# The last five spans of each layer of a two-layer GNN: edge rows added from SBUF pair by pair, one node stage between pairs, slot sums in one portion

## The chip, the cores and the metric

The kernel runs on one core of one Trainium2 chip. The metric is the device time of one execution in microseconds, taken as the median of several executions. The core has a matrix engine (TensorE, shown as PE, its weight loads as PEld), a vector engine (VectorE, DVE), an activation engine (ScalarE, ACT), GpSimd (POOL), which issues the indirect DMAs here, and SyncE (SP), which issues the other DMAs. Each engine works through its own queue in program order and waits on semaphores for the others. Tiles live in SBUF (128 partitions) or in PSUM, the banks that PE accumulates into.

## The reference

The graph has 6250 nodes and 106250 directed edges (50000 drawn, their reverses, and one loop per node), sorted by destination. A row has 256 float32.

```python
# layer 0
msg = relu(x[src] + edge_attr)
agg = segment_sum(msg, dst)
h = x + (x + agg)
f = gelu(bn1(h) @ W1.T + b1) @ W2.T + b2
x = layernorm(x + bn2(h + f))
# layer 1
h = gelu((x[src] + edge_attr) @ W1m + b1m)
agg = segment_sum(h @ W2m + b2m, dst) / max(deg, 1)
u = gelu(agg @ W1u + b1u) @ W2u + b2u
x = layernorm(x + layernorm_gamma_beta(x + u))
```

## The kernel before

**Tiles, spans, blocks.** The edges make 831 tiles of 128. Eight tiles are a span; there are V = 104 spans, 0 to 103, of which the last has seven tiles, the last of them with 10 rows. A span is two groups `g` of four tiles, a group two pairs `q`; so a span has four pairs, each a 128x512 operand. The 6250 nodes make 26 blocks of mostly 256 nodes. The last two, 24 and 25, have 128 and 96. A block is full when the last span with one of its edges has been summed: blocks 20 to 25 are full with spans 88, 92, 96, 100, 102 and 103.

**What is done to a span.** `gather` (L829) issues eight indirect DMAs from POOL, one a tile, which bring the row of each edge's source into `rings[v % 5]`, one of five ring buffers. The edge rows `ea` come by plain DMAs on SP's queue, three spans ahead (AHEAD). In layer 0 these are the raw edge features and the gathered rows those of x. In layer 1 the gathered rows are `proj` = (layer 0's result) @ W1m + b1m, and the edge rows needed are edge_attr @ W1m. The product is taken for the first group of every span during layer 0 and kept in DRAM (`zst`), and for the second group in layer 1 itself (`turned` L843/L848, `product` L856). The spans that are treated outside the steps, and the first three, have both groups' products ready in DRAM (`products_ahead`, `zst1`), and their edge rows can be added as they are. `one_hots` (L907, DVE, eight instructions) marks for each edge which of 32 slots its node has; `add_to_gathered` (L884, DVE) adds edge rows to gathered rows; `activated` or `activated_pair` (L892, L898, ACT) applies relu or gelu; `into_slots` (L927, PE) multiplies by the one-hots and so sums edges into slots; `kept_slots` (L946, ACT) copies the sums to SBUF; `slot_nodes` (L916, DVE) and `into_blocks` (L966, L974, PE) spread the slots over the nodes of the blocks, in `acc`.

**What is done to a full block.** A generator runs the node work in stages, and the list `running` holds those that are not finished. `nodes_0` is begun with two copies of `acc` (L1018 ACT, L1023 DVE) and the DMA of the degrees; its stages are: 1, W1 and gelu (L1029, L1034); 2, W2, residuals and statistics (L1042, L1047, L1052, L1054); 3, layernorm and the DMA of x1 (L1002, L1003, L1007); 4, the transpose (L1066, L1069); 5, the product with W1m, the add of b1m to `y` (L1075, L1079) and the DMA to `proj` (L1084, and L1086 for the last two blocks). `nodes_1` is begun with the division by the degree (L1347); its stages are A and B (L1357, L1362, L1367), the residuals (L1331, L1335), C (L1378, L1382 and statistics), D (L1388, L1392 and statistics), and E (the last scaling and the DMA to `out`, L1400).

**Order.** The order is written out by hand and kept. Spans 0 to 100 are gathered in steps (`step_0`, `step_1`): a step gathers span v, adds and activates span v-1, sums the second group of v-2, spreads v-3 and advances the running blocks. In the steps ACT lifts the edge rows into PSUM (`lifted`, L867) and DVE adds from there. Behind the steps come `end_0` and `end_1`. For spans 100 to 102, `late_step` calls `summed`: all one-hots, then four pairs raised into PSUM by PE against an identity (`raised`, L875, 16 matmuls of 256 columns), four adds, four activations, then the slot sums pair by pair with `further()`, which advances every running block by a stage, ahead of pairs 1 and 3. Then comes another `further()` and the spreading of the span (`full`).

**Between the layers.** Layer 1's gathers need `proj`. The gathers of its spans 0 to 2 read only `proj[:near+1]`, the rows of blocks 0 to 23, so they wait for the y of block 23. The rows of blocks 24 and 25 are added afterwards: `where(i)` loads the source numbers of one group into `tiles` or `off` and DVE builds a one-hot `z` from it (L1250), and `completed` multiplies that with y of blocks 24 and 25 and adds. The gathers from span 3 on read all of `proj` and wait for the y of block 25. Behind `full_0(103)`, `end_0` issues `where(0)`, `where(1)`, the stages of blocks 24 (`other`) and 25 (`last`) in turn, and in between `added(0)`, the lift and add of layer 1's span 0.

**Ring.** A gather into a ring buffer waits for the slot sums of the span five before.

Of the kernel before, what the change touches and what calls it, by code (L numbers as in the profile page):

```python
# [15 lines left out]
D = 256  # L16
# [11 lines left out]
RING = 5  # L28
ROW = 260
AHEAD = 3  # L30
LATE = 3
FIRST = 64


# [471 lines left out]
def kernel(  # L506
# [141 lines left out]
    with (  # L648
# [17 lines left out]
        def work():  # L666
            return psw.tile([P, 2, D], F32, name="workP")
# [199 lines left out]
                nc.scalar.copy(ps[:n, j:k, :], of[:n, q + j : q + k, :])  # L867
            return ps

        def raised(v, g, q, of):  # L870

            pair = tiles_of(v, g)[q : q + 2]
            ps = work()
            for j, n in enumerate(pair):
                nc.tensor.matmul(  # L875
                    ps[:n, j, :], lhsT=ident[:n, :n], rhs=of[:n, q + j, :], start=True, stop=True
                )
            return ps

        def add_to_gathered(v, g, q, ps):  # L880
            at = g * G + q
            r = rings[v % RING]
# [50 lines left out]
        def slot_bank():  # L933
            return pss.tile([P, 2 * D], F32, name="slotP")
# [222 lines left out]
                nc.sync.dma_start(out=zst[v], in_=zs.pop(v).rearrange("p j d -> p (j d)"))  # L1157
            advance(late)

        QUADS = [(g, q) for g in range(GROUPS) for q in range(0, G, 2)]  # L1160

        def summed(v, width, func, between=lambda i: None):

            one_hots(v)
            slot_nodes(v)
            its = [i for i in QUADS if tiles_of(v, i[0])[i[1] :]]
            rows = [raised(v, g, q, eas[v, g]) for g, q in its]
            for (g, q), ps in zip(its, rows):
                add_to_gathered(v, g, q, ps)
                activated_pair(v, g, q, func)  # L1170
            ps = slot_bank()
            for i, (g, q) in enumerate(its):
                between(i)
                at = g * G + q
                slots_of(v, width, ps, range(at, at + len(tiles_of(v, g)[q : q + 2])))
            kept_slots(v, ps, width)

        def further():
            advance(list(running))

        def late_step(v, full, func, width):

            u = v - 1
            if v == V - LATE:
                full(u - 2)
                activated(u - 1, 1, func)
                slot_nodes(u - 1)
                kept_slots(u - 1, into_slots(u - 1, width), width)
                further()
                full(u - 1)  # L1190
            summed(u, width, func, lambda i: further() if i % 2 else None)
            further()
            full(u)

        def kept_of(v):

# [33 lines left out]

        wheres = []

        def added(v):
            for g, q in QUADS:
                add_to_gathered(v, g, q, lifted(v, g, q, eas[v, g]))

        def where(i):

            to = check.tile([P, T], F32, name=("tiles", "off")[i % 2])[:, : G * P]
            nc.sync.dma_start(
                out=to,
                in_=src_rows[i * G : (i + 1) * G, :].rearrange("t e -> (t e)")[None, :]
                .to_broadcast([P, G * P]),
            )
            hot = ep.tile([P, G, D], F32, name="z", bufs=2).rearrange("p g d -> p (g d)")
            hot = hot.rearrange("p (b e) -> p b e", e=G * P)
            for b in range(len(LAST)):
                nc.vector.tensor_scalar(  # L1250
                    hot[:, b, :], to, -float(near + sum(LAST[:b])), place,
                    op0=ALU.add, op1=ALU.is_equal,
                )
            wheres.append(hot)
# [13 lines left out]
        def end_0():  # L1268

            d = V - 1  # L1270
            for v in range(V - LATE, V):
                gather(v, x, src_sb)
                late_step(v, full_0, AF.Relu, D + 1)
            other = list(running)[-1]
            assert len(running) == 1 and len(farther) == 0
            for v in range(AHEAD):
                gather(v, proj[: near + 1, :], src_near)
                load_1(v)
            summed(d, D + 1, AF.Relu, lambda i: further() if i % 2 == 0 else None)
            full_0(d, acc_work)  # L1280
            last = list(running)[-1]
            assert len(running) == 2
            advance([last])
            for i in (0, 1):
                where(i)
            for _ in range(3):
                advance([other])
                advance([last])
            added(0)
            further()  # L1290
            further()
            assert not running and len(farther) == len(LAST)
            added(1)


# [153 lines left out]
            prepared[b] = nodes_1(b, *its, bank, True)  # L1449
            next(prepared[b])  # L1450

        def full_1(v, bank=node_work, last=False):
            for b in into_blocks(v, acc_1, opened_1):
                if last:
                    gen = prepared.pop(b)
                else:
                    gen = nodes_1(b, acc_1[b], x1s.pop(b), degs_1.pop(b), invs.pop(b), bank, last)
                del acc_1[b]
                begun(b, gen)
            invert()  # L1460

        def step_1(v):
            u, w, full = v - 1, v - 2, v - 3
            if v + AHEAD < V:
                load_1(v + AHEAD)
            if AHEAD <= v:
                gather(v, proj, src_1)
            some, early_edges = AHEAD <= u, 0 <= u < AHEAD
            if early_edges:
# [12 lines left out]
            if some:  # L1482
                add_to_gathered(u, 0, 0, lifted(u, 0, 0, eas[u, 0]))
                add_to_gathered(u, 0, 2, lifted(u, 0, 2, eas[u, 0]))
            if early_edges:
                completed(u, 0)
                if u + 1 < AHEAD:
                    where(2 * u + 2)
            advance(early)
            if some:  # L1490
                add_to_gathered(u, 1, 0, product(*first))
            if early_edges:
                completed(u, 1)
                if u + 1 < AHEAD:
                    where(2 * u + 3)
            if 0 <= u:
                activated(u, 0, AF.Gelu)
            if 0 <= w < V:
                slot_nodes(w)
                kept_slots(w, into_slots(w, D), D)  # L1500
            if some:
                add_to_gathered(u, 1, 2, product(*second))
            advance(late)

        def end_1():

            d = V - 1
            for v in range(V - LATE, V):
                gather(v, proj, src_1)
                if v == V - 1:  # L1510
                    for b, bank in zip(sorted(acc_1), (node_work, acc_work)):
                        prepare(b, bank)
                late_step(v, lambda u: full_1(u, last=u == d - 1), AF.Gelu, D)
            assert len(running) == 1
            other = running[0]
            summed(d, D, AF.Gelu, lambda i: further() if i < 3 else None)
            full_1(d, last=True)
            last = running[-1]
            advance([last])
            advance([last])  # L1520
            while running:
                advance(list(running))

        begin()
        for v in range(AHEAD):
# [5 lines left out]
        for v in range(V - LATE):  # L1531
            step_0(v)
            beside.get(v, lambda: None)()
            if v > 8 and v % 2:
                next(ahead_0, None)
        assert next(ahead_0, "none") == "none"
        end_0()
        for v in range(V - LATE):
            step_1(v)
# [64 lines left out]
```

## Time and profile before

| What | Value |
|---|---|
| median of 3 runs | 2167.87 us (2167.82 to 2168.67) |
| profiled execution | 2165.82 us |
| its span in the trace | 2163.9 us |
| mean granted TensorE clock | 0.968 |
| PE busy | 1903.9 us (88%) |
| DVE busy | 1451.8 us (67%) |
| ACT busy | 1341.3 us (62%) |
| POOL busy | 1583.8 us (73%) |

The profile is one execution; it is 1.9 us longer than its span, as time lies around the first and last recorded instruction. Its page lists the busy time of each engine, the span in 40 slices, the chain of waits that ended last and the costliest groups of instructions. In a group's line `out<-in` names the tiles, `x` the count, and the figures behind the bar are busy time, mean ns of one, and idle time ahead of them with what ended most of it.

The last sums of a span into slots leave for SBUF in `kept_slots` (L946). In the trace this copy ends, for spans 98 to 103, at 1010.7, 1016.8, 1031.4, 1047.75, 1059.5 and 1071.4 us in layer 0, and at 2076.5, 2082.5, 2098.7, 2117.2, 2132.3 and 2146.9 us in layer 1. The last DVE instruction ends at 2158.6 us, the span 5.3 us after that.

### The profile page before, as it was taken

The numbers are of one execution on the slowest core, as the hardware profiler recorded it, in microseconds if no ns is written. First come the engines' busy times: TensorE is split into PE (matmuls) and PEld (weight loads), VectorE is DVE, ScalarE is ACT, GpSimd is POOL, SyncE is SP. The second block draws the span as 40 slices with busy tenths as digits, with TensorE's granted clock in tenths as the row PEclk, the third lists the DMA queues.
The fourth block names the chain that finished last, engine by engine and source line by source line (L and its number), as shares of the span: only waits on it lengthen the run. The fifth ranks groups of instructions, "written<-read, shape, count | busy, mean of one in ns | idle before, by whom it ended". The sixth has DMA issues, their size and how long they took to land.

```text
span 2163.9 us, 38059 instructions
## 1 busy us (share of the span) xinstructions
PE 1903.9 (88%) x12071; PEld 1472.0 (68%) x12071; DVE 1451.8 (67%) x4205; ACT 1341.3 (62%) x2153; POOL 1583.8 (73%) x1671
## 2 busy tenths in 40 slices
PE   5999999998998989898779998898888988888886
PEld 3777767776776777666557776677766766766654
DVE  6677766776776667666366766676676766666665
ACT  3577766676766666665336766665665666666653
POOL 7777777777777777777567777777777777777770
PEclk9999999999999999999989999999999999999998
DMA  9889888888988898887568777777777767777650
GB/s 335 263 290 323 293 294 290 292 287 286 301 289 283 287 295 281 286 288 243 174 206 267 225 244 233 221 238 243 227 227 228 242 213 235 219 233 227 212 167 26
DMA packets 318430, 541.75 MB, mean 250 GB/s; under 512 B 37260, under 2 KB 234125, under 8 KB 318093
## 3 DMA queue, kind: packets, MB, share of 16 engines
q1 hardware_dynamic: 237773, 319.65, 44.3%
q0 software_dynamic: 79744, 217.71, 32.6%
q8 instruction: 99, 1.62, 0.3%
q10 hardware_dynamic: 704, 1.87, 0.2%
q14 instruction: 110, 0.90, 0.1%
HBM read 461.90 MB, written 77.18 MB: 249 GB/s over the span
## 4 chain that ended last, share of the span: by engine, by line
PE 21%; DMA 12%; DVE 8%; issue 6%; ACT 4%; POOL 3%; DVEq 0%; ACTq 0%; POOLq 0%
DMA ring<-proj,dst_sb 11%; PE workP L856 8%; POOL ring L829 3%; PE slotP L927 3%; DVE ring L884 2%; PE nodeP L1378 2%; PE acc L966 2%; PE nodeP L1357 2%; DVE hot L907 2%; PE workP L843 1%; DVE uT L1362 1%; ACT ring L892 1%; ACT L1002 1%; PE workP L1262 1%; ACT workP L867 1%
## 5 line engine op out<-in xcount | busy, mean ns | idle before, releaser
L829 POOL DMA_INDIRECT ring<-in_x_dram,src_sb x831 | 789.0, 949 | 255.6 <-issue 137.3
L829 POOL DMA_INDIRECT ring<-proj,dst_sb x807 | 769.9, 954 | 252.8 <-issue 152.3
L856 PE MATMUL workP<-w1m_sb,eaT 128*128 128x256 f32 x3324 | 830.0, 395 | 67.8 <-DVE ring L884 45.4
L884 DVE TENSOR_TENSOR ring<-workP,ring 128x512 f32<-128x512 f32 x844 | 557.2, 684 | 426.8 <-DMA ring<-in_x_dram,src_sb 126.0
L856 PEld LDWEIGHTS workP<-w1m_sb,eaT 128*128 128x128 f32 x3324 | 621.1, 195 | 237.2 <-DVE ring L884 58.3
L892 ACT ACTIVATE ring<-ring 128x1024 f32<-128x1024 f32 x400 | 424.8, 1062 | 147.7 <-DVE ring L884 144.7
L848 ACT COPY eaT<-workP 128x512 f32<-128x512 f32 x416 | 223.8, 585 | 262.7 <-PE workP L843 261.6
L867 ACT COPY workP<-ea 128x512 f32<-128x512 f32 x606 | 334.0, 595 | 32.0 <-DVE ring L884 30.6
L966 PE MATMUL acc<-hot,sums 128*128 128x161 f32 (+22 forms) x1376 | 225.1, 296 | 91.5 <-DVE hot L960 48.9
L907 DVE TENSOR_SCALAR hot<-ramp,slot 128x32 f32<-128x32 f32 x1662 | 268.1, 259 | 0.2 <-PE slotP L927 0.2
L966 PEld LDWEIGHTS acc<-hot,sums 128*128 128x128 f32 x1376 | 187.0, 195 | 110.6 <-DVE hot L960 53.9
L927 PE MATMUL slotP<-ring,hot 128*32 128x257 f32 (+1 forms) x3324 | 248.6, 388 | 12.0 <-ACT ring L892 6.2
L843 PE MATMUL workP<-ident,ea 128*128 128x128 f32 x1584 | 212.3, 276 | 15.8 <-DMA ea<-in_edge_attr_dram 8.6
L843 PEld LDWEIGHTS workP<-ident,ea 128*128 128x128 f32 x1584 | 186.2, 142 | 41.1 <-issue 10.6
L927 PEld LDWEIGHTS slotP<-ring,hot 128*32 128x32 f32 x3324 | 97.7, 109 | 129.2 <-issue 63.3
L946 ACT COPY sums<-slotP 128x257 f32<-128x257 f32 (+1 forms) x208 | 75.4, 362 | 134.4 <-PE slotP L927 134.4
L1367 ACT ACTIVATE uT<-uT,cols_sb 128x256 f32<-128x256 f32 (+3 forms) x104 | 45.8, 487 | 132.5 <-DVE uT L1362 132.4
L1357 PE MATMUL nodeP<-fT,w 128*128 128x256 f32 (+2 forms) x400 | 101.5, 400 | 25.6 <-DVE y L1392 25.2
L1357 PEld LDWEIGHTS nodeP<-fT,w 128*128 128x128 f32 x400 | 77.9, 204 | 45.6 <-DVE y L1392 32.1
L1002 ACT ACT_TABLE_LOAD x73 | 93.7, 1283 | 1.3
L1378 PE MATMUL nodeP<-w2u_sb,uT 128*128 128x256 f32 (+1 forms) x392 | 89.3, 381 | 1.4 <-DVE y L1335 1.4
L1156 DVE COPY z<-workP 128x512 f32<-128x512 f32 x101 | 69.1, 684 | 20.7 <-PE workP L856 20.0
(154 smaller groups left out, 1582.5 us busy)
## 6 DMA issues: line engine op xcount, KB each, us to landing
ea<-in_edge_attr_dram SPq DMA_DIRECT2D x103, 1024.0 KB
ea<-zst SPq DMA_DIRECT2D x110, 512.0 KB
zst<-z SPq DMA_DIRECT2D x101, 512.0 KB
ea<-in_edge_attr_dram SPq DMA_DIRECT2D x97, 512.0 KB
ring<-in_x_dram,src_sb POOLq DMA_INDIRECT x831
ring<-proj,dst_sb POOLq DMA_INDIRECT x807
xb<-in_x_dram SPq DMA_DIRECT2D x23, 256.0 KB
x1d<-x SPq DMA_DIRECT2D x23, 256.0 KB
```

Of the source, the lines that this page charges most:

```text
L829: nc.gpsimd.indirect_dma_start(out=rings[v % RING][:n, j, :D], out_offset=None, in_=table, in_offset=bass.IndirectOffsetOnAxis(ap=rows[:n, ...
L843: nc.tensor.transpose(pe[:, j, k, :n], ea[:n, at + j, k * P : (k + 1) * P], ident[:n, :n])
L848: nc.scalar.copy(eaT[:, j:k, :, :n], pe[:, j:k, :, :n])
L856: nc.tensor.matmul(ph[:n, j, :], lhsT=eaT[:, j, k, :n], rhs=w1m_sb[:, k, :], start=(k == 0), stop=(k == KC - 1),)
L867: nc.scalar.copy(ps[:n, j:k, :], of[:n, q + j : q + k, :])
L884: nc.vector.tensor_add(r[:n, at + j : at + k, :D], ps[:n, j:k, :], r[:n, at + j : at + k, :D])
L892: nc.scalar.activation(at, at, func)
L907: nc.vector.tensor_scalar(hots[v][:n, j, :], ramp[:n, :SLOTS], slot[:n, t : t + 1], None, op0=ALU.is_equal,)
L927: nc.tensor.matmul(ps[q * SLOTS : (q + 1) * SLOTS, :width], lhsT=hot[:n, j, :], rhs=r[:n, j, :width], start=(i == 0), stop=(i == PAIR - 1 ...
L966: nc.tensor.matmul(acc[b][:, k, cols], lhsT=its[:, k * P : (k + 1) * P], rhs=at, start=(begins and k == 0), stop=(last_span[b] == v and k ...
L1357: nc.tensor.matmul(ps[:, o - i, :width], lhsT=w12[:, k, o * P : (o + 1) * P], rhs=mT[:, k, :width], start=(k == 0), stop=(k == KC - 1),)
L1378: nc.tensor.matmul(ps[:n, h, :], lhsT=uT[:, k, h * n : (h + 1) * n], rhs=w2u_sb[:, k, :], start=(k == 0), stop=(k == UC - 1),)
```

## The change

LATE goes from 3 to 4, so the steps end with span 99, and the spans 99 to 103 of each layer are treated in a new function, `late_spans`. In it

- `raised`, the PE matmuls that put edge rows into PSUM, is gone; DVE adds the edge rows from SBUF, a pair at a time, with the pair's activation behind it;
- behind each pair `between` runs one stage of the oldest running block (`stage`); behind pair 0 first `full` of the span before, behind pair 3 first the one-hots of the next span;
- the slot sums of a span come in one portion behind its four pairs (`into_slots`);
- the gather of span v+1 is issued ahead of the pairs of span v;
- in layer 0 `where` is split into its DMA (`where`) and its one-hots (`whose`); the loads 0 and 1 go out in the last step but one, and those behind them in span 100 and in layer 1's step 1;
- in layer 0 `added(0)` comes behind the last stage of blocks 24 and 25, and these two alternate by themselves;
- in layer 1 `prepare`, the residuals of blocks 24 and 25, goes behind pairs 2 and 3 of span 102, and the last stages of both blocks alternate;
- one more span per layer has its second group's product made ahead: `products_ahead` makes 14 pairs in layer 0 instead of 12 and 10 in layer 1 instead of 8, one phase of a pair in every odd step.

```diff
-LATE = 3
+LATE = 4
...
-        def raised(v, g, q, of):
...
-        def summed(v, width, func, between=lambda i: None):
-
-            one_hots(v)
-            slot_nodes(v)
-            its = [i for i in QUADS if tiles_of(v, i[0])[i[1] :]]
-            rows = [raised(v, g, q, eas[v, g]) for g, q in its]
-            for (g, q), ps in zip(its, rows):
-                add_to_gathered(v, g, q, ps)
-                activated_pair(v, g, q, func)
-            ps = slot_bank()
-            for i, (g, q) in enumerate(its):
-                between(i)
-                at = g * G + q
-                slots_of(v, width, ps, range(at, at + len(tiles_of(v, g)[q : q + 2])))
-            kept_slots(v, ps, width)
-
-        def further():
-            advance(list(running))
...
+        def stage():
+
+            if running:
+                advance(running[:1])
+
+        def late_spans(load, table, rows, full, func, width, between, behind=lambda v: None):
+
+            v = V - LATE
+            for u in range(v + AHEAD, V):
+                load(u)
+            gather(v, table, rows)
+            full(v - 3)
+            activated(v - 2, 1, func)
+            slot_nodes(v - 2)
+            kept_slots(v - 2, into_slots(v - 2, width), width)
+            one_hots(v - 1)
+            for v in range(V - LATE - 1, V):
+                if v + 1 < V:
+                    gather(v + 1, table, rows)
+                for i, (g, q) in enumerate(PAIRS):
+                    if tiles_of(v, g)[q:]:
+                        add_to_gathered(v, g, q, eas[v, g][:, q : q + 2, :])
+                        activated_pair(v, g, q, func)
+                    if i == 0:
+                        full(v - 1)
+                    if i == 3 and v + 1 < V:
+                        one_hots(v + 1)
+                    between(v, i)
+                slot_nodes(v)
+                kept_slots(v, into_slots(v, width), width)
+                behind(v)
...
+            def between(v, i):
+                if v == V - LATE and i > 1:
+                    whose()
+                    where(i)
+                if v < d or i < 2:
+                    stage()
...
+            late_spans(load_0, x, src_sb, full_0, AF.Relu, D + 1, between, behind)
+            full_0(d, work)
+            other, last = running
             advance([last])
-            for i in (0, 1):
-                where(i)
-            for _ in range(3):
+            for _ in range(2):
                 advance([other])
                 advance([last])
+            advance([other])
+            advance([last])
+            advance([last])
+            assert not running and len(farther) == len(LAST)
             added(0)
-            further()
-            further()
             added(1)
...
+            def between(v, i):
+                if v == d - 1 and i > 1:
+                    prepare(sorted(acc_1)[i - 2], work)
+                elif v < d or i < 3:
+                    stage()
+
+            late_spans(load_1, proj, src_1, lambda v: full_1(v, v >= d - 1), AF.Gelu, D, between)
+            full_1(d, True)
+            other, last = running
+            for gen in (last, last, other, last, other, last, last):
+                advance([gen])
```

More of the change, by code (lines that the diff above doesn't have):

```diff
@@ L868, in lifted @@
             return ps
-        def raised(v, g, q, of):
[L872 to L878, printed above, removed]
         def add_to_gathered(v, g, q, ps):
@@ L1158, in step_0 @@
             advance(late)
-        QUADS = [(g, q) for g in range(GROUPS) for q in range(0, G, 2)]
-        def summed(v, width, func, between=lambda i: None):
-            one_hots(v)
-            slot_nodes(v)
-            its = [i for i in QUADS if tiles_of(v, i[0])[i[1] :]]
-            rows = [raised(v, g, q, eas[v, g]) for g, q in its]
-            for (g, q), ps in zip(its, rows):
-                add_to_gathered(v, g, q, ps)
-                activated_pair(v, g, q, func)
-            ps = slot_bank()
-            for i, (g, q) in enumerate(its):
-                between(i)
-                at = g * G + q
-                slots_of(v, width, ps, range(at, at + len(tiles_of(v, g)[q : q + 2])))
-            kept_slots(v, ps, width)
@@ L1178, in further @@
-        def further():
-            advance(list(running))
[L1181 to L1188, printed above, removed]
-                further()
-                full(u - 1)
-            summed(u, width, func, lambda i: further() if i % 2 else None)
-            further()
-            full(u)
+        PAIRS = [(g, q) for g in range(GROUPS) for q in range(0, G, 2)]
@@ L1229 @@
         ahead_1 = products_ahead([(v, 1) for v in range(V - LATE - 1, V)])
-        wheres = []
+        froms, wheres = [], []
         def added(v):
-            for g, q in QUADS:
+            for g, q in PAIRS:
                 add_to_gathered(v, g, q, lifted(v, g, q, eas[v, g]))
@@ L1246, in where, with whose @@
             )
+            froms.append(to)
+        def whose():
+            to = froms.pop(0)
             hot = ep.tile([P, G, D], F32, name="z", bufs=2).rearrange("p g d -> p (g d)")
@@ L1270, in end_0, with behind @@
             d = V - 1
[L1271 to L1282, printed above, removed]
+            def between(v, i):
[4 more added lines that the diff above has]
+                    stage()
+                if (v, i) == (d - 1, 3):
+                    assert not running and not farther
+            def behind(v):
+                if v == d - 1:
+                    for u in range(AHEAD):
+                        gather(u, proj[: near + 1, :], src_near)
+                        load_1(u)
+            late_spans(load_0, x, src_sb, full_0, AF.Relu, D + 1, between, behind)
+            full_0(d, work)
+            other, last = running
             advance([last])
-            for i in (0, 1):
-                where(i)
-            for _ in range(3):
+            for _ in range(2):
                 advance([other])
                 advance([last])
+            advance([other])
+            advance([last])
+            advance([last])
+            assert not running and len(farther) == len(LAST)
             added(0)
-            further()
-            further()
-            assert not running and len(farther) == len(LAST)
             added(1)
@@ L1450, in prepare, with full_1 @@
             next(prepared[b])
-        def full_1(v, bank=node_work, last=False):
+        def full_1(v, last=False):
             for b in into_blocks(v, acc_1, opened_1):
@@ L1456, in full_1 @@
                 else:
-                    gen = nodes_1(b, acc_1[b], x1s.pop(b), degs_1.pop(b), invs.pop(b), bank, last)
+                    gen = nodes_1(b, acc_1[b], x1s.pop(b), degs_1.pop(b), invs.pop(b), node_work, last)
                 del acc_1[b]
@@ L1487, in step_1 @@
                 if u + 1 < AHEAD:
-                    where(2 * u + 2)
+                    whose()
+                    if u + 2 < AHEAD:
+                        where(2 * u + 4)
             advance(early)
@@ L1494, in step_1 @@
                 if u + 1 < AHEAD:
-                    where(2 * u + 3)
+                    whose()
+                    if u + 2 < AHEAD:
+                        where(2 * u + 5)
             if 0 <= u:
@@ L1507, in end_1 @@
             d = V - 1
[L1508 to L1522, printed above, removed]
+            def between(v, i):
[8 more added lines that the diff above has]
+                advance([gen])
+            assert not running
         begin()
@@ L1535 @@
                 next(ahead_0, None)
-        assert next(ahead_0, "none") == "none"
+            if v == V - LATE - 2:
+                assert next(ahead_0, "none") == "none"
+                where(0)
+                where(1)
         end_0()
```

## The prediction

> **What bounds the kernel now.** I read the slices first (every engine is below 90% nearly everywhere, so no engine's total sets the time), then the groups, then POOL's timeline, then DVE's and PE's at both ends of a layer.
>
> ```profile
> L829 POOL DMA_INDIRECT ring<-in_x_dram,src_sb x831 | 789.0, 949 | 255.6 <-issue 137.3
> L829 POOL DMA_INDIRECT ring<-proj,dst_sb x807 | 769.9, 954 | 252.8 <-issue 152.3
> ```
>
> A gather costs POOL 0.95 us and 0.30 of issue behind it, 1.25 us. A span's eight make 10.0 us, and they follow one another without a break through the steps. Work inside the steps is therefore free as long as it keeps up. Time is lost where POOL waits:
>
> ```profile
> 1046.21 0.89 POOL L829 DMA_INDIRECT ring<-in_x_dram,src_sb  x1 [0.30 <-issue]
> 1061.84 0.98 POOL L829 DMA_INDIRECT ring<-proj,src_near  x1 [14.75 <-DMA degd<-degs]
> ...
> 1094.94 0.94 POOL L829 DMA_INDIRECT ring<-proj,dst_sb  x1 [3.05 <-DMA proj<-y]
> 1098.06 0.94 POOL L829 DMA_INDIRECT ring<-proj,dst_sb  x1 [2.18 <-PE workP L1262]
> ...
> 1129.66 0.94 POOL L829 DMA_INDIRECT ring<-proj,dst_sb  x1 [2.68 <-issue]
> ...
> 2113.71 0.87 POOL L829 DMA_INDIRECT ring<-proj,dst_sb  x1 [0.30 <-DVE uT L1362]
> ```
>
> Layer 0's last gather is at 1046.2. Layer 1's first waits 14.75 us (for y of block 23, whose add ends at 1058.8; the DMA named beside it is long done). Its span 3 starts at 1094.94, 3.4 us after y of block 25 (added at 1091.15 to 1091.56). Its span 6 starts at 1129.66, 38.1 us after that y: it needs the ring buffer of span 1, whose sums need the completion by blocks 24 and 25. From 1129.66 POOL doesn't stop until 2113.71, and the span ends 50.2 us after that. So two chains count: **up to y of block 25** (each us saved there moves 1129.66 and all behind it) and **the tail behind the last gather**. The tail isn't waiting for rows:
>
> ```profile
> 2105.46 2.47 DVE L884 TENSOR_TENSOR ring<-workP,ring 128x512 f32<-128x512 f32 x4
> ...
> 2138.07 2.20 DVE L884 TENSOR_TENSOR ring<-workP,ring 128x512 f32<-128x512 f32 x4
> ```
>
> These are the adds of spans 101 and 103. The last gathers of these spans were issued at 2095.9 and 2113.7, 9.6 and 24.4 us before, while rows land some 2 to 6 us after issue. The tail is one in-order chain of small operations.
>
> **What the change removes.** (1) `raised`: 16 matmuls, 3.64 us a span on PE (99.76 to 103.4 in span 101 of layer 1), work that lies ahead of the adds but beside DVE. (2) Slot sums by pairs, 4 x 1.05 us (warm, two tiles each), become one portion, 1.07 to 1.20 us for eight tiles. (3) In layer 0, the wait for source numbers:
>
> ```profile
> 1073.04 0.36 DVE L1023 COPY hT<-acc 128x192 f32<-128x192 f32 x1 [0.28 <-ACT fT L1018]
> 1081.62 0.88 DVE L1250 TENSOR_SCALAR z<-tiles,place 128x512 f32<-128x512 f32 x2 [8.22 <-DMA tiles<-src_rows]
> ```
>
> DVE stands for 8.22 us with blocks 24 and 25 queued behind it, then spends some 1.9 on four one-hots (the first two 0.88), and later 2.5 on `added(0)`. All this lay between kept(103) at 1071.4 and y of block 25 at 1091.56, 20.2 us. In the changed order the two loads go out about 25 us before use, the one-hots lie in span 100, and `added(0)` follows the y. What is left by rows: spreading 1.5, copies 0.7, then stages of block 25 back to back with block 24's between: 1.4 + 0.8 (stage 1, half width), 1.6 + 2.0 (2), 1.0 (3), 0.5 + 0.5 (4), 1.0 + 0.4 (5): 11.4 to 12.4 us. The chain therefore gives **8 us** here, if kept(103) stays put.
>
> **What it adds.** (4) Twenty adds per layer from two SBUF operands in place of PSUM and SBUF. No row has that at 128x512. The nearest stand in the weights' preparation:
>
> ```profile
> 31.38 0.42 DVE L791 TENSOR_TENSOR bn_s<-bn_s,rows_sb 128x256 f32<-128x256 f32 x1
> 31.73 0.41 DVE L792 TENSOR_TENSOR bn_b<-rows_sb 128x256 f32<-128x256 f32 x1
> ```
>
> 0.42 for 256 columns is what the PSUM form takes for 256 (0.41 at L1335), so I take 0.68 for 512, the PSUM form's. The gathers beside these rows stay at 0.95 (one of four 1.11); beside other DVE work on 128x831 at 48 to 55 us they took 1.14 to 1.45. Upper bound: 0.5 us on each gather beside an add, 10 a layer, 5 us of POOL, hidden by the rows' lead of 9.6 us and more; lower bound nothing. I take nothing. The Trainium skill, "SBUF — State Buffer", section "Who interferes with whom", speaks against the change: by it a VectorE tensor_tensor with both inputs in SBUF locks the port that GpSimd's SBUF reads use. The rows at 31 us don't show it; by the rule every add would hold up a gather that it meets, and the sum would stand higher by what of it isn't covered, up to 14 us over both layers.
>
> (5) Stages in series. Before, `further` issues a stage of each running block, whose PE, ACT and DVE parts overlap with the slot sums. Now each stage stands between two pairs, and the next add queues on DVE behind the stage's DVE work, which waits for its PE and ACT. Span 100 of layer 1, by rows: add and activation 0.69 + 0.61; residuals 0.58 + 1.37; C 3.72 on PE and 1.9 on DVE; add, activation 1.3; table load 1.28, root 0.3, D 3.2 on DVE; add, activation 1.3; slot sums 1.07, copy 0.36 = 17.7, and with semaphore hops of some 0.05 to 0.1 between engines 18.3. Before it was 16.2 (2082.5 to 2098.7).
>
> I walked both orders so through all late spans, each instruction with its row's duration, started when its engine and its inputs are free. For layer 1, the last DVE instruction comes out at 2162.4 for the old order (measured 2158.6: the walk is 3.8 late, on both sides) and 2163.7 for the new: **+1.3**. For layer 0, kept(103) is at 1075.2 for the old (measured 1071.4) and 1070.6 for the new, so 4.6 earlier: span 99 comes out 5.6 late (its add and sums lose their step), and spans 102 and 103 win it back, as neither raising nor sums by pairs stand in them. Together with the stretch of 11.4 to 12.4, y of block 25 comes at 1078.3 in place of 1091.56, **-13.3**. Layer 1's starts follow: span 0 at y of block 23 plus 3.0, 1056 to 1061; span 6, 38.1 behind y of block 25.
>
> (6) The clock. With `raised` gone PE pauses more: in the walk four gaps of 4 to 12 us in layer 1's tail and five of 3.4 to 6.7 in layer 0's, against three of 3.2 to 3.8 and none. What a gap costs, before:
>
> ```profile
> 2106.85 1.91 PE L927 MATMUL slotP<-ring,hot 128*32 128x256 f32 x4 [3.45 <-ACT ring L898]
> 2108.70 3.78 PE L1357 MATMUL nodeP<-fT,w 128*128 128x256 f32 x8
> 2112.41 1.20 PE L927 MATMUL slotP<-ring,hot 128*32 128x256 f32 x8
> 2113.54 1.99 PE L1357 MATMUL nodeP<-fT,w 128*128 128x256 f32 x8
> ```
>
> After 3.45 us of idling the same eight matmuls take 3.78 in place of 1.99, and the granted clock of the stretch is 0.62:
>
> ```profile
> 2086.00:2104.00 18.00, 15.40 (x76) 11.63 (x76) 11.54 (x34) 6.56 (x11) 13.52 (x15) 1.00 0.41 117
> 2104.00:2112.00 8.00, 5.15 (x12) 3.06 (x12) 5.00 (x17) 5.28 (x7) 6.18 (x7) 0.62 0.39 112
> ```
>
> At 2 us per such gap on the chain, layer 0's gain shrinks from 13.3 to 4.7 and layer 1's tail goes from +1.3 to +5.0.
>
> (7) Two more pairs made ahead per layer: steps with such work take 10.09 us, those without 10.05; 12 more steps, +0.5 us.
>
> Sum: warm -13.3 + 1.3 + 0.5 = -11.5; every gap cold -4.7 + 5.0 + 0.5 = +0.8. I take the middle, -5: 2165.8 - 5 = 2161 for a run like the profiled one, **2163** at the median, which is 2 above it.
>
> **The rivals.**
> - **Slower: PE stays cold through the late spans.** If the stages in series keep PE so idle that the clock lies at 0.7 throughout both ends (before: 0.62 to 1.00, 0.90 on average over 2086 to 2152), all PE rows grow 1.4-fold. Walked so, y of block 25 comes 0.5 us later than before and the tail ends 11.4 later: 2168 + 12 = 2180. At 0.8 it is -5.2 + 7.6, so 2170. By straight line between these it is slower than before from 0.83 down, and by more than 0.2% from 0.78. For it: the gaps. Against it: L1357 and L1378 make the longer stages dense.
> - **Rows as they land.** The title's idea taken at its word: each span done soon after its rows, the tail then some 25 us behind the last gather in place of 50: 2168 - 8 - 20 = 2140. Against it: the adds of span 103 ran 24 us after the last issue because of the queue, and the walk has the new queue no shorter.
> - **No net change.** Layer 0's gain comes out cold (-5) and layer 1's tail gives it back: 2168.
> - **The lock.** If each of some 10 adds a layer holds up a gather by its own 0.68 us, and if the rows' lead doesn't cover it: 7 us a layer on top of the forecast, 2163 + 14 = 2177. Against it: the lead of 9.6 us, and the rows at 31 us.
>
> **How the numbers follow.** Small gain as walked, 0.38; no net change 0.22; cold clock or lock 0.31; rows as they land 0.09. The measurement tells 0.2%, 4.3 us, from no change. Faster than that: 0.47 (0.38 and 0.09); same 0.22; slower 0.31. The range goes from 2150 (warm, and a little of the second rival) to 2177 (a clock of 0.75); the forecast's own is 2156 to 2168.
>
> **What would show it.** Right: no 8 us wait ahead of L1250; y of block 25 at 1078 to 1087; POOL's break ahead of layer 1's span 6 gone 5 to 13 us earlier; 16.5 to 18.5 us between kept(99) and kept(100) in layer 1; the last gather to the end 51 to 56 us. Wrong: a granted clock under 0.8 over the last 70 us; adds of L884 far over 0.68; gathers over 1.1 us beside them; or a new POOL wait in the steps.

## The result and the profile after

The changed kernel takes 2184.54 us (median of 6 runs, 2175.74 to 2185.97), the kernel before beside it 2167.47; the ratio is 1.0072 (95% interval 1.0054 to 1.0090), so it is slower by 0.7%, some 15.6 us. The forecast was 2163 in a range of 2150 to 2177. The profiled execution took 2185.75 us with a span of 2184.0, 20.1 longer than before's span, at a clock of 0.948 (0.968). In four of the later sets of runs the kernel before itself took 2794 to 2858 us; of these only the ratio, with a wide interval, and distances at the end of layer 1 are used, which for one and the same kernel differ by 0.5 to 2.8 us between sets.

The head of the page of the changed kernel and its two groups of gathers:

```profile
span 2184.0 us, 37829 instructions
...
L829 POOL DMA_INDIRECT ring<-in_x_dram,src_sb x839 | 798.5, 952 | 257.8 <-issue 144.7
L829 POOL DMA_INDIRECT ring<-proj,dst_sb x815 | 779.4, 956 | 249.3 <-issue 151.8
```

The counts are the first surprise: 839 and 815 gathers, 831 and 807 before. In `late_spans` the line ahead of the loop gathers span 100, and the loop's first round, v = 99, gathers v + 1 = 100 again. Eight gathers at 1.25 us are 10.0 us of POOL in each layer. The prediction had no term for them.

POOL's timeline of the changed kernel, where it waits and where it ends:

```profile
1068.66 1.19 POOL L829 DMA_INDIRECT ring<-proj,src_near  x1 [9.97 <-PE slotP L917]
...
1130.86 0.94 POOL L829 DMA_INDIRECT ring<-proj,dst_sb  x1 [1.32 <-issue]
...
2126.66 0.88 POOL L829 DMA_INDIRECT ring<-proj,dst_sb  x1 [0.30 <-DVE ring L874]
```

Layer 1's first gather is at 1068.66 (1061.84 before) and span 6's at 1130.86 (1129.66). The last one is at 2126.66, 12.95 later than before, and the end lies 57.3 behind it in place of 50.2. y of block 25 is 3.0 us later (1094.52 against 1091.56), but POOL starts span 6 only 1.2 later. The 20.1 us are thus 1.2 from that start, 10.0 of second gathers, 1.75 of other delay among the gathers up to the last one, and 7.1 behind it.

Seen from the sums rather than from POOL, all of it arises late in layer 1: `kept_slots` of span 98 ends at 2074.75, 1.75 *earlier* than before, and from there to the last DVE instruction it is 103.7 us where it was 82.1. These are ACT's copies for spans 99 to 103 in the changed kernel:

```profile
2091.32 0.37 ACT L936 COPY sums<-slotP 128x256 f32<-128x256 f32 x1 [0.49 <-PE slotP L917]
2113.77 0.37 ACT L936 COPY sums<-slotP 128x256 f32<-128x256 f32 x1 [0.45 <-PE slotP L917]
2137.05 0.37 ACT L936 COPY sums<-slotP 128x256 f32<-128x256 f32 x1 [6.78 <-PE slotP L917]
2153.54 0.37 ACT L936 COPY sums<-slotP 128x256 f32<-128x256 f32 x1 [1.79 <-PE slotP L917]
2164.65 0.37 ACT L936 COPY sums<-slotP 128x256 f32<-128x256 f32 x1 [1.39 <-PE slotP L917]
```

Span 99, which the steps of before finished 6.0 us behind span 98, now takes 16.9; spans 100 and 101 take 22.4 and 23.3 (16.2 and 18.5 before). DVE shows what a pair waits for:

```profile
2093.01 0.69 DVE L874 TENSOR_TENSOR ring<-ea,ring 128x512 f32<-128x512 f32 x1 [2.52 <-DMA ring<-proj,dst_sb]
...
2120.31 0.87 DVE L1362 SCALAR_TENSOR_TENSOR uT<-degb,b,nodeP 128x256 f32<-128x256 f32 x2 [3.88 <-PE nodeP L1357]
2121.10 0.68 DVE L874 TENSOR_TENSOR ring<-ea,ring 128x512 f32<-128x512 f32 x1
2125.06 0.87 DVE L1362 SCALAR_TENSOR_TENSOR uT<-degb,b,nodeP 128x256 f32<-128x256 f32 x2 [3.27 <-PE nodeP L1357]
```

The first add of span 100 waits 2.52 us for the rows of the second issue. In span 101 each add (L874) stands behind a stage's DVE part, and that behind the stage's matmuls. The last row is a window: its bounds and length, then PE, PEld, DVE, ACT and POOL busy with their instructions, the granted clock, the DMA share and GB/s. The clock is 0.65; it was 0.87 over the same 90 us before:

```profile
2080.00:2170.00 90.00, 55.85 (x218) 37.15 (x218) 43.46 (x130) 34.83 (x57) 36.26 (x38) 0.65 0.24 73
```

### The profile page after: what moved, and what is told of

It reads as the page before. It is cut to its first block, busy times and chain, and to the rows that moved or that the text cites. A ratio compares the mean times of both kernels' runs of the same rounds, so it can differ in the third digit from the quotient of the medians.

```text
span 2184.0 us, 37829 instructions
## 1 busy us (share of the span) xinstructions
PE 1898.1 (87%) x11947; PEld 1460.8 (67%) x11947; DVE 1452.6 (67%) x4207; ACT 1342.7 (61%) x2153; POOL 1602.9 (73%) x1687
## 4 chain that ended last, share of the span: by engine, by line
PE 21%; DMA 14%; DVE 7%; issue 6%; ACT 5%; POOL 3%; DVEq 0%; ACTq 0%; POOLq 0%
DMA ring<-proj,dst_sb 13%; PE workP L856 9%; POOL ring L829 3%; PE slotP L917 3%; PE acc L956 3%; PE nodeP L1378 2%; DVE ring L874 2%; PE nodeP L1357 2%; DVE hot L897 1%; PE workP L843 1%; ACT L992 1%; ACT ring L882 1%; DVE uT L1362 1%; ACT workP L867 1%; ACT eaT L848 1%
## 5 line engine op out<-in xcount | busy, mean ns | idle before, releaser
L829 POOL DMA_INDIRECT ring<-in_x_dram,src_sb x839 | 798.5, 952 | 257.8 <-issue 144.7
L829 POOL DMA_INDIRECT ring<-proj,dst_sb x815 | 779.4, 956 | 249.3 <-issue 151.8
L874 DVE TENSOR_TENSOR ring<-workP,ring 128x512 f32<-128x512 f32 x804 | 533.6, 685 | 430.1 <-DMA ring<-in_x_dram,src_sb 131.7
L848 ACT COPY eaT<-workP 128x512 f32<-128x512 f32 (+1 forms) x416 | 223.4, 585 | 266.0 <-PE workP L843 265.1
L956 PE MATMUL acc<-hot,sums 128*128 128x161 f32 (+22 forms) x1376 | 232.6, 303 | 97.8 <-DVE hot L950 51.0
L956 PEld LDWEIGHTS acc<-hot,sums 128*128 128x128 f32 x1376 | 192.0, 200 | 122.2 <-DVE hot L950 56.0
L1357 PE MATMUL nodeP<-fT,w 128*128 128x256 f32 (+1 forms) x384 | 102.5, 415 | 31.4 <-DVE y L1392 27.7
L1378 PEld LDWEIGHTS nodeP<-w2u_sb,uT 128*128 128x128 f32 (+1 forms) x384 | 74.3, 198 | 17.4 <-issue 4.8
```

The source lines that it names most:

```text
L829: nc.gpsimd.indirect_dma_start(out=rings[v % RING][:n, j, :D], out_offset=None, in_=table, in_offset=bass.IndirectOffsetOnAxis(ap=rows[:n, ...
L848: nc.scalar.copy(eaT[:, j:k, :, :n], pe[:, j:k, :, :n])
L874: nc.vector.tensor_add(r[:n, at + j : at + k, :D], ps[:n, j:k, :], r[:n, at + j : at + k, :D])
L956: nc.tensor.matmul(acc[b][:, k, cols], lhsT=its[:, k * P : (k + 1) * P], rhs=at, start=(begins and k == 0), stop=(last_span[b] == v and k ...
L1357: nc.tensor.matmul(ps[:, o - i, :width], lhsT=w12[:, k, o * P : (o + 1) * P], rhs=mT[:, k, :width], start=(k == 0), stop=(k == KC - 1),)
L1378: nc.tensor.matmul(ps[:n, h, :], lhsT=uT[:, k, h * n : (h + 1) * n], rhs=w2u_sb[:, k, :], start=(k == 0), stop=(k == UC - 1),)
```

## The experiments

Theories after this result: the **doubled gathers**; the **cold clock**; **stages in series**, which make a span outside the steps dear; and the **port lock** of the adds from SBUF. "Tail" below is the time from `kept_slots` of span 98, or of span 99, to the last DVE instruction of layer 1.

### Without the second issue

```diff
-                if v + 1 < V:
+                if V - LATE < v + 1 < V:
                     gather(v + 1, table, rows)
```

> The changed kernel issues 1654 gathers, 16 more than before: span 100 of each layer is gathered twice. This kernel drops the second issue. Cold-clock theory (PE pauses more than 3 us between stages, so the stages run at half clock): the doubled gathers cost only what span 100's first add waits for them in layer 1 (2.52 us) and some disturbance in layer 0; 2179 to 2183, granted clock of the last 70 us still under 0.75. Rival, the doubled gathers are the loss (10 us of POOL in each layer): about 2165.

> As the first time, in which the kernel before itself took 2813 us, so that its runs say little: the changed kernel without the second issue of span 100's gathers. Cold-clock theory: 2179 to 2183, granted clock of the last 70 us under 0.75. Doubled gathers are the loss: about 2165.

The first time: 1.0013 of before (0.9963 to 1.0064), which tells nothing. The second: 2178.41 us, ratio 1.0050 (1.0034 to 1.0067). The tail from span 98 falls from 103.7 to 95.5 us, of which span 100 gives 4.3 (22.4 to 18.1). So the second issue isn't the main loss: the interval overlaps that of the changed kernel, and a gain of about 0.2% is likely but not separated. POOL had room, as before's own rows ran 9.6 us ahead of use in span 101.

> The changed kernel itself, beside the next two on one chip: 1.0054 to 1.009 of the kernel before, as measured first. If the doubled gathers cost nothing, as the first two intervals (1.0072 with, 1.0050 without) still allow, 1.005.

1.014 (1.0053 to 1.0228): slower again, too wide to size the second issue. Its tail from span 99 is 84.0 us, against 81.1 in the first run without the second issue.

### Keeping PE warm

```diff
+        def filled(times):
+            ps = work()
+            for _ in range(times):
+                for j in range(2):
+                    nc.tensor.matmul(ps[:, j, :], lhsT=ident, rhs=w1m_sb[:, j, :], start=True, stop=True)
...
                     between(v, i)
+                    filled(5)
```

> The changed kernel with ten matmuls of 256 columns (some 2.3 us at full clock), whose result nobody reads, behind the stage after each pair of the late spans. Cold-clock theory: granted clock of the last 70 us up from 0.65 to 0.85 or more, kept(100) to kept(101) in layer 1 down from 23.3 to 18 us, 2162 to 2174. Rival, the doubled gathers are the loss: no change, 2184. Rival, the stages in series cost this at any clock: 2180 to 2190, the clock up and the stages' distances as they were.

> Both edits. Cold-clock theory: 2158 to 2170, 2 to 5 below the filler alone. Doubled gathers alone: as without the second issue, about 2165. Stages in series at any clock: 2176 to 2186.

1.0377 (1.0295 to 1.0460) and 1.0337 (1.0248 to 1.0425). The filler was twice what its expectation says, 20 instructions a pair, and PE was busy 77.8 of 80 us with it at the end of the first. These two are mis-sized and test none of the theories.

With `filled(2)`:

> The same with a smaller filler: two times two matmul calls behind each pair, which make 8 matmul instructions of about 0.23 us, 1.8 us a pair (the first filler was 20 instructions, 4.6 us a pair, 18 us a span, and PE was 97% busy with it at both ends). Cold-clock theory: granted clock of the last 70 us over 0.85, kept(100) to kept(101) in layer 1 18 us in place of 23.3, 2160 to 2172 in all. Stages in series at any clock: 2176 to 2186.

2184.98 us, 1.0081 (1.0063 to 1.0099), no faster than without filler, at a clock of 0.91 over 2080 to 2170. PE's timeline of span 101, first without filler, then with it:

```profile
2127.52 6.45 PE L1378 MATMUL nodeP<-w2u_sb,uT 128*128 128x256 f32 x16 [4.13 <-DVE y L1335]
2133.90 1.08 PE L917 MATMUL slotP<-ring,hot 128*32 128x256 f32 x16
```

```profile
2130.15 3.69 PE L1386 MATMUL nodeP<-w2u_sb,uT 128*128 128x256 f32 x16 [0.67 <-DVE y L1343]
2133.68 1.89 PE L875 MATMUL workP<-w1m_sb,ident 128*128 128x256 f32 x8
2135.50 1.07 PE L924 MATMUL slotP<-ring,hot 128*32 128x256 f32 x16
```

Stage C falls from 6.45 to 3.69 us, and 1.8 of it goes to the filler that stands ahead of the slot sums (L875). Added over stages A, B and C of the tail, matmuls take 11.2 us more than their warm rows without filler and 4.1 with it; the tail from span 98 is 98.9 us in place of 95.5. So these matmuls are mostly warm, and the filler still costs more than that gives.

> The changed kernel without the second issue, with a filler only where PE has nothing to do next: 8 matmul instructions (1.8 us) behind stage B and stage 2, 12 (2.8 us) behind C and D, 4 behind stages 1, 3 and the last ones, none elsewhere. Cold-clock theory: clock over 0.85 at both ends, A and B 2.0 us and C 3.7 us in place of 3 to 3.8 and 6.5, no stage of PE later than without filler; 2163 to 2172. Stages in series at any clock: 2174 to 2182, kept(98) to kept(103) still some 74 us in layer 0 (before 60.7).

> As the first time, in which the kernel before itself took 2858 us, so that its runs say little: without the second issue, with the filler only where PE has nothing to do next. Cold-clock theory: clock over 0.85 at both ends, 2163 to 2172. Stages in series at any clock: 2174 to 2182, kept(98) to kept(103) in layer 0 still some 74 us (before 60.7).

With the filler aimed at the gaps (each stage hands back how much may follow it): 1.0147 (1.0097 to 1.0197) and then 2184.40 us, 1.0070 (1.0053 to 1.0087), at a clock of 0.86. It didn't do all it was meant to: A and C of span 101 still took 3.78 and 5.32 us. `kept_slots` of spans 98 to 103 of layer 0 lay 69.2 us apart (60.7 before, 74.4 without filler). No filler made the kernel faster; what a warm PE would give for nothing stays open. The 11.2 us are what stages A to C of layer 1's tail lose, on the chain or beside it.

### One late span less

```diff
-LATE = 4
+LATE = 3
```

with the second issue gone, the last stages of blocks 24 and 25 in turn as their number asks, and by the new LATE two pairs of products fewer made ahead in each layer.

> The changed kernel without the second issue and with LATE = 3: span 99 stays in the steps, four spans instead of five come late. Stages in series: a late span takes 16 to 18 us whatever its rows do, a span of the steps 10, so each layer gains 5 to 9 us; 2161 to 2170. Cold-clock theory: the remaining four spans stay as cold; only the pauses of one span go, 2172 to 2177.

> Without the second issue and with LATE = 3, so four late spans in place of five. Stages in series: each layer gains 5 to 9 us, 2161 to 2170. Cold-clock theory: 2172 to 2177.

1.0043 (0.9987 to 1.0099), then 2170.73 us, ratio 0.9998 (0.9982 to 1.0013): the loss is gone. The interval lies clear of the 1.0050 (1.0034 to 1.0067) with five late spans, and the clock over 2080 to 2170 is still 0.73. ACT's copies for spans 98 and 99 with LATE = 3, then with 4:

```profile
2080.34 0.35 ACT L936 COPY sums<-slotP 128x256 f32<-128x256 f32 x1
2086.51 0.37 ACT L936 COPY sums<-slotP 128x256 f32<-128x256 f32 x1 [1.27 <-PE slotP L917]
```

```profile
2080.57 0.37 ACT L936 COPY sums<-slotP 128x256 f32<-128x256 f32 x1 [2.14 <-PE slotP L917]
2096.62 0.37 ACT L936 COPY sums<-slotP 128x256 f32<-128x256 f32 x1
```

6.17 against 16.05 us: a span that the steps finish in the shadow of the next one takes a whole round of four stages outside them. The tail from span 98 is 86.1 us in place of 95.5. A warmer PE explains little of that: matmuls of stages A to C of the tail take 9.9 us more than their warm rows here, 11.2 with five late spans. Most of the gain lies in layer 1. In layer 0 the sums of spans 98 to 103 are still 72.1 us apart, against 74.4 with five late spans and 60.7 before. So neither layer's end is back where it was (86.1 against 82.1 us in layer 1); what makes up for it in time may be the gain at the layer boundary, which no run separates in this order.

### The adds: from where, and in which order

> Without the second issue of span 100's gathers, and each pair's edge rows raised into PSUM by PE (4 matmuls) ahead of its add, which then reads PSUM. Cold-clock theory: PE gets only 0.9 us per pair, the pauses stay mostly over 3 us; within 5 us of the kernel without the second issue. Port-lock theory (adds from two SBUF operands hold up gathers): no gather of the late spans over 1.1 us, and 7 us or more faster than the kernel without the second issue.

(`raised` per pair, the add from PSUM.) 1.0151 (1.0080 to 1.0222), beside 1.0013 without it in the same set; slower rather than faster. No gather of its last 125 us takes over 1.1 us, but none does without `raised` in that set either, so the lock isn't tested by it.

The kernel before, with its late adds from SBUF:

```diff
-            rows = [raised(v, g, q, eas[v, g]) for g, q in its]
+            rows = [eas[v, g][:, q : q + 2, :] for g, q in its]
```

> The kernel before with nothing changed but the adds of spans 100 to 103: from SBUF, PE doesn't raise. Cold-clock theory: without 3.6 us of PE a span the clock falls from 0.87 to 0.75 or less over 2080 to 2170 and the time rises by 4 to 12 us, 2169 to 2177. Stages in series: the order is the old one, so no loss; 2158 to 2166. Port-lock theory: gathers of spans 101 to 103 over 1.1 us where adds run.

> The kernel before with only the adds of spans 100 to 103 from SBUF and no raising. Cold-clock theory: the clock over 2080 to 2170 falls from 0.87 to 0.75 or less, 2169 to 2177. Stages in series: 2158 to 2166. Port-lock theory: gathers of spans 101 to 103 over 1.1 us.

0.9974 (0.9922 to 1.0027), then 2175.22 us, 1.0022 (1.0010 to 1.0034). The clock over 2080 to 2170 fell to 0.82, less far than the cold-clock theory said, the tail from span 98 stayed (82.5 against 82.1), and yet the kernel is 0.2% slower. POOL shows the lock. Its rows, and DVE's row of the same moment:

```profile
1026.36 3.30 POOL L829 DMA_INDIRECT ring<-in_x_dram,src_sb  x1 [0.30 <-issue]
...
2112.40 2.98 POOL L829 DMA_INDIRECT ring<-proj,dst_sb  x1 [0.31 <-issue]
```

```profile
1026.35 2.48 DVE L884 TENSOR_TENSOR ring<-ea,ring 128x512 f32<-128x512 f32 x4
```

A gather that begins with four adds in a row takes 3.30 us in place of 0.95: it ends 0.83 us after they have ended. Five gathers of this trace met such a run, one of them a shorter one, and took 9.2 us more than 0.95 each. In the kernel before, whose adds at the same places read PSUM, no gather of the late spans takes over 1.1 us.

The kernel before, with its late slot sums in one portion:

```diff
-                between(i)
-                at = g * G + q
-                slots_of(v, width, ps, range(at, at + len(tiles_of(v, g)[q : q + 2])))
-            kept_slots(v, ps, width)
+                between(i)
+            kept_slots(v, into_slots(v, width), width)
```

> The kernel before with nothing changed but the slot sums of spans 100 to 103 in one portion behind both advances. Stages in series: the sums wait for both stages, no work of PE lies between them, 0 to +6 us. If sums by pairs only cost time (4.2 against 1.1 us a span): -4 to -10 us.

1.0027 (0.9962 to 1.0093): open. Its tail from span 99 is 81.7 us (76.1 before), which would agree with the first theory, from one trace.

The adds of a late span ahead of its stages:

> The changed kernel without the second issue, the four adds and activations of a late span issued one after another, the four stages behind them, with no add between stages. If adds queued behind stages cost the time: they ran late only because of the queue, and a span gets 2 to 4 us shorter, 10 to 20 us per layer, 1.000 or less. If it is the stages themselves in series (each of the four waits for the one before): the span keeps 15 to 18 us, 1.004 to 1.007.

```diff
                         activated_pair(v, g, q, func)
+                for i, (g, q) in enumerate(PAIRS):
                     if i == 0:
                         full(v - 1)
```

1.0027 (0.9990 to 1.0065), between the two ranges. The tail from span 99 is 75.4 us, 81.1 and 79.5 with an add between stages. The trace shows a reason neither theory had: ACT loads its tables 5 times in this tail instead of 9, as gelu no longer comes between the roots of stages D and E; four loads of 1.28 us are 5.1 us.

> LATE = 3 without the second issue (0.9998 of before), and in each late span the four adds and activations ahead of the four stages. If adds queued behind stages cost time: each late span shorter by 1 us or more, kept(99) to the last DVE instruction in layer 1 some 74 us in place of 79, 0.994 to 0.998. If it is the stages in series alone: 0.999 to 1.002, the distance as it was.

1.0004 (0.9952 to 1.0056), unsettled in time. The tail from span 99 is 74.8 us, in an execution of 2830.81 us where the median was 2801.62; without the edit it is 79.9 and 81.1, with 13 table loads for 9. So the order of adds has its share, about 5 us in both kernels, which is what four table loads sum to; whether the adds' place in the queue costs anything besides isn't told apart, and a better time is not shown.

### The layer boundary alone

On the kernel before: `where` split from its one-hots, its loads in step 99, the one-hots behind span 102, and `added(0)` moved:

```diff
             other = list(running)[-1]
             assert len(running) == 1 and len(farther) == 0
+            whose()
+            whose()
...
             advance([last])
-            for i in (0, 1):
-                where(i)
...
-            added(0)
             further()
             further()
             assert not running and len(farther) == len(LAST)
+            added(0)
```

> The kernel before with only the layer boundary's part of the change: the two loads of source numbers go out in the last step but one, their four one-hots behind span 102, the lift and add of layer 1's span 0 behind the last stage of blocks 24 and 25. If the 8.2 us wait on the loads was on the path (as the prediction says): no DVE wait ahead of the one-hots, y of block 25 some 10 us earlier, gathers of layer 1's span 6 some 8 to 12 us earlier, 2155 to 2160. If the wait was covered (blocks 24 and 25 bound by PE and the cold clock after the pause): 2164 to 2168.

2160.85 us, ratio 0.9980 (0.9970 to 0.9990): faster than both kernels. DVE's timeline there:

```profile
1062.24 0.86 DVE L1255 TENSOR_SCALAR z<-tiles,place 128x512 f32<-128x512 f32 x2
...
1084.33 0.42 DVE L1079 TENSOR_TENSOR y<-acc,rows_sb 96x256 f32<-96x256 f32 x1 [2.74 <-PE acc L1075]
```

The 8.22 us wait is gone, y of block 25 ends at 1084.75 in place of 1091.56, and the last gather starts at 2107.07 in place of 2113.71: 6.8 and 6.6 us.

> The kernel with only the layer boundary's part of the change (0.998 of before) and LATE = 2 in place of 3: spans 101 to 103 late, span 100 in the steps. If every span that is taken out of the steps costs 5 us or more per layer, as LATE = 3 in place of 4 gave 11 us in the changed order: 0.992 to 0.996. If the old order with its two stages at a time doesn't pay for a late span: 0.997 to 1.000.

0.9991 (0.9941 to 1.0042): the old order with one late span less was not told apart from no change.

## Why the prediction was wrong

Of its own signs of being wrong two showed: a granted clock of 0.65 over the last 70 us, and gathers of up to 1.44 us beside the adds.

- **Removal (3), right.** From kept(103) to y of block 25 it took 13.4 us in the changed kernel and 11.3 with the boundary alone; 11.4 to 12.4 was said, 20.1 it was. The gain that POOL saw was 6.6 us by itself; in the changed kernel it was overrun by a kept(103) that came at 1081.15. y of block 23 came late as well, so that layer 1's first gather was at 1068.66, where 1056 to 1061 was said, and span 6's at 1130.86, 1.2 later than before instead of 13.3 earlier. Without the second issue POOL doesn't wait at all between these two (1073.01 and 1134.09), so there the first gather sets the start of span 6.
- **Removal (1), nothing gained.** The prediction had this work beside DVE. Without raising, the tail of the old order stayed (82.5 against 82.1), and the time rose by 0.2%.
- **What was left out.** The change issues span 100's gathers twice. The prediction has no term for that: 10 us of POOL per layer, 8.2 us in the tail's traces, some 0.2% in time.
- **Step (5), the failing one.** It said +1.3 for layer 1's tail and 4.6 earlier for kept(103). Without the doubled gathers the tail from span 98 is 13.4 longer than before and kept(98) to kept(103) of layer 0 is 13.7 longer (74.4 to 60.7). Span 100 of layer 1, the one worked out by rows, was right: 18.3 us said, 18.1 measured without the second issue. What failed is the price of span 99, the fifth outside the steps. The walk had it 5.6 late in layer 0 and let spans 102 and 103 win that back; it came 10.5 later behind span 98 in layer 0 and 10.1 in layer 1, and spans 102 and 103 together won back 0.6 and 2.1. LATE = 3 shows the price by itself: 9.9 us for span 99 of layer 1, and 0.5% of the time. The walk came out 3.8 late for the old order and this was taken to hold "on both sides", which it did not: for the new one it came out short.
- **Step (6), too small.** The sum took half of what 2 us per gap would cost: +1.8 in layer 1's tail on top of the warm walk. How 8.6 and 3.7 us follow from five and one more gaps at 2 us each isn't worked out there. Stages A to C of layer 1's tail took 17.0 us more than their warm rows in the changed kernel and 11.2 without the second issue, 1.8 before; how much of that lies on the chain isn't shown. The rival of the cold clock gave 2180 at 0.7, and 0.65 was measured with 2184.5. Its number was near, in part by luck, as the second issue is in it and was not in the rival. The clock isn't shown as the cause: at 0.73, with 9.9 us of such matmul time, the kernel with LATE = 3 has no loss, and raising the clock by filler won nothing. It may still be part of the price of each late span.
- **Step (7), small.** 0.5 us was said for the products made ahead. From span 6 of layer 1 to the last gather it is 987.3 us without the second issue, 985.7 with LATE = 3 and 984.0 before, which bounds it at some 3 us a layer.
- **Step (4), the wrong choice between its ends.** The adds cost 0.68 us as taken (38 full ones, 680 ns). Gathers beside them do stand. The Trainium skill, "SBUF — State Buffer", section "Who interferes with whom", has it that a VectorE instruction with two SBUF inputs contends with a GpSimd instruction that reads SBUF. The gather of 3.30 us agrees. Why the rows at 31 us, with adds of 0.42 us, don't show it is open. In the changed kernel, pair by pair, it costs little: the mean gather goes from 949 to 952 and from 954 to 956 ns, 4.1 us over both layers, of which 2.6 lie in the late spans, where 14 was the bound.

In trace terms the tail's 21.6 us are 8.2 for the second issue, 9.4 for the fifth span and 4.0 for the rest, taken in this order, each from one trace. These executions took 1.2, 5.1 and 3.2 us more than their medians, and before's 1.7 less, so the ratios of the times are the better measure: 0.2% for the second issue, not separated from nothing, and 0.5% for the fifth span.

## What to carry to other kernels

Count every DMA issue of both kernels before anything else: a duplicate is visible in the diff and changes no result. A span that a pipeline finishes in the shadow of the next one should not leave the pipeline early; outside it, it took 16 us in place of 6 here, and an activation put between two stages of another function adds a table load each way, 1.28 us each here. When two orders are walked by hand, a bias found on one of them need not hold for the other: the difference is no better known than the sum.

## What was not expected of the hardware

A gather that starts within a run of SBUF-to-SBUF adds on DVE ends some 0.8 us behind the run: it took 3.30, 2.69, 2.43 and 2.98 us in four cases at runs of 2.48 us, and 1.44 at one add of 0.68, against 0.95 alone. Behind a pause PE can be slow for a whole stage: 16 matmuls took 6.45 us behind a pause of 4.13, at a granted clock of 0.56, and 3.72 behind one of 1.41.
